# Two ordering ties on VectorE in a four-layer graph network: ranking steps behind the expert's additions, and a combine's later additions behind the first normalised nodes

## The chip, the cores and the metric

The kernel runs on one core of one Trainium2 chip. The metric is the device time of one execution in microseconds (us), as the median of several. One core has five engines that run their own instruction streams in order: TensorE (PE in the profile; its weight loads are listed as PEld), VectorE (DVE), ScalarE (ACT), GpSimd (POOL) and SyncE (SP), which here only issues transfers. They wait for one another by semaphores. ScalarE and GpSimd issue transfers as well. Matrix products land in PSUM, in a pool of eight tiles that is shared by the whole program.

## The reference, cut to what matters

The graph has 3125 nodes with 256 features and 50000 weighted edges, sorted by destination. Four pairs of layers follow one another, each pair a graph convolution and a feed-forward layer. With `A[dst, src]` the sum of the edge weights and `C[dst, src]` the number of edges between two nodes, the parts that the change touches are these:

```
x = A @ (x @ W) + b                            # convolution 0

w   = x @ wr + br                              # gated expert layer (0)
sel = the 1561 nodes with the largest w        # of equal ones the lower index
y   = gelu(x @ w1 + b1) @ w2 + b2
x   = x + (w * y where sel, 0 elsewhere)

h   = norm(x) @ W_pre ...                      # convolution 1: two products with C,
                                               # scaled by the degrees
x   = x + ...; top-2 of 8 experts; x = x + z0 + z1   # feed-forward layer 1

h   = norm(x)                                  # convolution 2: four products with A
...
```

Ahead of each convolution but the first, `x` is normalised by layer norm without gain: each node's mean is subtracted and the result is divided by its standard deviation. In layer 1 each node goes to two experts; `z0` and `z1` are the two weighted results, a row of 256 values per node each. Further layers (three and the rest of two) aren't touched.

## The kernel before, in words

**Data.** The nodes are 25 tiles of 128 (`NT`; the last holds 53 nodes). `x` stays in SBUF with nodes on the partitions. `CHUNKS` are groups of four node tiles: six of four and one of one. GpSimd builds dense 3200 x 3200 tables of `A` (`tw`) and `C` (`tcn`) in DRAM by indirect scatters (L595), a few hundred each; those of `tcn` run through the gated expert layer and beyond, to 904.8 us. A convolution streams the table from DRAM through SyncE's queue and multiplies it with `h` (L265 where the result has features on the partitions, L305 where it has nodes there). The program holds two arms for edges that are sorted or not; here the sorted one runs.

**The gated expert layer** (`l0_ffn`, from L967). Here *all* nodes go through the expert, and the selection is applied afterwards. For each group, `expert` (L933) does the following.

- Eight hidden blocks: two matmuls (L941) into one PSUM tile, four passes in the trace's count, then the Gelu (L945) on ScalarE.
- One product per node tile: eight matmuls (64 in the trace for four tiles, L952), then `take`, which is the addition `y = ps + b2` on VectorE (L1016). It hands the PSUM tile back.

Beside it runs the generator `ranks` (L994). For each of the 25 node tiles it counts how many nodes of all have a larger `w`: two or three comparisons over a row of 3200 with an accumulated sum (L1000), and one over 128 for ties (L1004). `expert` takes a step of it at two of the eight hidden blocks and at two of the four node tiles; what is left over after the last group is run there. The sum (L1009) and the gate `s` (L1010) follow, and then 25 updates of `x` (L1022), one for each node tile. VectorE has all of these in one queue. `self.pace` hands the last addition of a group to the generator of the scatters: the next portion of GpSimd's scatters is tied behind it.

**From there to the second convolution** (`l1_gnn`, L1056). `norm` (L173) works in fives of node tiles: statistics (L163 and L164), the root on ScalarE (L168, tied behind the last Gelu), the reciprocal (L171) and five normalisations (L184). For each group, TensorE then transposes (L225), VectorE and ScalarE copy (L230, L232), TensorE projects (L345), VectorE adds a bias (L1074), ScalarE scales (L1075), and `split` (L317 to L319) makes the high and low parts with which L265 multiplies the first table.

**The combine** (end of `Experts.tiles`, from L2012). The two results per node lie in DRAM (`L_ffn_z`). Nine parts of 1, 1, 2, 4, 4, 4, 4, 4 and 1 node tiles are fetched on ScalarE's queue (L2023) into a ring of three buffers, `zt`. Two additions per part (L2039) put them on `x`; then `part` of `norm_parts` (L189) computes statistics (L201, L202), the root on ScalarE (L203), the reciprocal (L204) and the normalisations (L206). The third convolution, `spmm_rows` (L287), multiplies them with the table `tw`, node tile by node tile (L305). Its table loads after the first are tied behind the transfers of the parts whose nodes they serve.

**What sets the order.** The source order isn't the order of the engines' queues. A scheduler in the framework places each instruction by its estimate of when it can start, under the dependencies that it knows. `order(a, b, sync=False)` adds one such dependency by hand: `a` is placed after `b`. Between two instructions of one engine it needs no semaphore and only fixes their order in the queue.

Of the kernel before, what the change touches and what calls it, by code (L numbers as in the profile page):

```python
# [60 lines left out]
class Net:  # L61
# [127 lines left out]
    def norm_parts(self, name):  # L189

        nc, got, loads = self.nc, [], {}

        def part(t0, nt, load):
            loads[t0 + nt] = load
            if not got:
                got.append(self.nm_tile(name))
            mv = self.small.tile([P, 4, 2], F32, tag="mv4", name=self.name("mv"))
            rs = self.small.tile([P, 4], F32, tag="rs4", name=self.name("rs"))
            for i in range(nt):
                st = self.small.tile([P, 6], F32, tag="bn", name=self.name("bn"), bufs=4)  # L200
                nc.vector.bn_stats(st, self.x[:, t0 + i, :])  # L201
                nc.vector.bn_aggr(mv[:, i, :], st)  # L202
            nc.scalar.activation(rs[:, :nt], mv[:, :nt, 1], AF.Sqrt, bias=self.eps)  # L203
            nc.vector.reciprocal(rs[:, :nt], rs[:, :nt])  # L204
            for i in range(nt):
                nc.vector.tensor_scalar(  # L206
                    got[0][:, t0 + i, :],
                    self.x[:, t0 + i, :],
                    mv[:, i, 0:1],
                    rs[:, i : i + 1],  # L210
                    op0=ALU.subtract,
                    op1=ALU.mult,
                )

        return lambda: (got[0], loads), part

# [750 lines left out]
    def l0_ffn(self, fm, w, w1, w2):  # L967

        nc, ins = self.nc, self.ins
        ht = 8  # L970
        take_k = max(1, int(0.5 * N))
        take_k = take_k - 1 if take_k > 1 else 1
        with self.reusing("l0f") as pool:
            b1 = self.columns(pool, ins["L0_ffn_b1"].rearrange("(r p) -> r p", p=P), ht)
            b2 = pool.tile([P, D], F32, name="b2")
            nc.sync.dma_start(b2, ins["L0_ffn_b2"].partition_broadcast(P))


            wp, low = pool.tile([P, NT], F32, name="score_p"), pool.tile([P, NT], F32, name="low")
            nc.vector.tensor_scalar(low, self.valid, -1.0, FMAX, op0=ALU.add, op1=ALU.mult)  # L980
            nc.vector.tensor_mul(wp, w, self.valid)
            nc.vector.tensor_add(wp, wp, low)
            row = pool.tile([P, NP], F32, name="score_row")
            self.broadcast_row(wp, row)

            after = pool.tile([P, P], F32, name="after")
            nc.vector.tensor_add(after, self.before, self.ident)
            nc.vector.tensor_scalar(after, after, 0.5, None, op0=ALU.is_lt)
            rk = pool.tile([P, NT, 4], F32, name="rk")
            nc.vector.memset(rk, 0.0)  # L990
            junk = pool.tile([P, NP], BF16, name="junk")
            rank, s = pool.tile([P, NT], F32, name="rank"), pool.tile([P, NT], F32, name="take")

            def ranks():  # L994
                for t in range(NT):
                    a, b = t * P, (t + 1) * P
                    me = wp[:, t : t + 1]
                    for i, (lo, hi, op) in enumerate(((0, a, ALU.is_ge), (b, NP, ALU.is_gt), (a, b, ALU.is_gt))):
                        if hi > lo:
                            nc.vector.tensor_scalar(  # L1000
                                junk[:, lo:hi], row[:, lo:hi], me, None, op0=op, op1=ALU.add,
                                accum_out=rk[:, t, i : i + 1],
                            )
                    nc.vector.scalar_tensor_tensor(  # L1004
                        junk[:, a:b], row[:, a:b], me, after, op0=ALU.is_equal, op1=ALU.mult,
                        accum_out=rk[:, t, 3:4],
                    )
                    yield
                nc.vector.tensor_reduce(rank, rk, AX.X, ALU.add)  # L1009
                nc.vector.scalar_tensor_tensor(s, rank, float(take_k), w, op0=ALU.is_lt, op1=ALU.mult)  # L1010

            y, steps, taken = self.nm_tile("y"), ranks(), []
            for t0, nt in CHUNKS:
                last = self.expert(
                    pool, fm[:, :, t0 * P : (t0 + nt) * P], nt * P, w1, b1, AF.Gelu_apprx_tanh, ht, w2,
                    lambda i, ps: taken.append(nc.vector.tensor_add(y[:, t0 + i, :], ps, b2)), steps,  # L1016
                )
                self.pace(taken[-1])
            for _ in steps:
                pass  # L1020
            for t in range(NT):
                nc.vector.scalar_tensor_tensor(  # L1022
                    self.x[:, t, :], y[:, t, :], s[:, t : t + 1], self.x[:, t, :], op0=ALU.mult, op1=ALU.add
                )
        return last
# [242 lines left out]
    def prefix(self, pool, t, n):  # L1268
# [7 lines left out]
        return t  # L1276

    def slot_owners(self, pool, slots, tiles):


# [10 lines left out]
        hot = self.nm_tile("hot").rearrange("p t d -> p (t d)").bitcast(BF16)  # L1291
        place = hot[:, : n * P].rearrange("p (n c) -> p n c", c=P)
        which = hot[:, n * P : n * (P + 2 * tiles)].rearrange("p (n s c) -> p n s c", s=2, c=tiles)
        ps = self.psum()[:, : 2 * tiles]
        step = 10 if n % 10 == 0 else 5
# [165 lines left out]
    def l3_ffn(self, late):  # L1461
# [54 lines left out]
        def rest():  # L1516
            with self.reusing("l3f") as pool:
# [36 lines left out]
                nc.vector.scalar_tensor_tensor(slot, slot, -none, kept, op0=ALU.add, op1=ALU.mult)  # L1554
                nc.vector.tensor_scalar(slot, slot, none, None, op0=ALU.add)
                number, place = self.slot_owners(pool, slot, NE * tiles)
                at, more = tile_("at", [P, NE * tiles]), tile_("more", [P, NE * tiles])
                of, to = tile_("of", [P, NE * tiles], I32), tile_("to", [P, NE * tiles], I32)
# [108 lines left out]
class Experts:  # L1667
# [253 lines left out]
    def tiles(self, pool, side, then):  # L1921
        net, nc, ins, tc = self.net, self.nc, self.ins, self.net.tc
# [45 lines left out]
        for i in range(STILES):  # L1968
# [40 lines left out]
            outs.append(st)  # L2009
            next(side, None)  # L2010

        bounds, back = [0, 1, 2] + list(range(4, NT, 4)) + [NT], []  # L2012
        if not summed:
            zt3 = net.nm_tile("zt")
            zts = [zt3[:, 8 * i : 8 * i + 8, :].rearrange("p (k t) d -> p k t d", k=2) for i in range(3)]
        for t0, t1 in zip(bounds, bounds[1:]):
            nt = t1 - t0
            x = net.x[:, t0:t1, :]
            full = nt if t1 < NT else nt - 1

            def fetch(dst, k):
                eng = nc.gpsimd if summed and t0 >= 2 else nc.scalar
                put = lambda d, s: back.append(eng.dma_start(d, s))  # L2023
                if full:
                    r = k * NP + t0 * P
                    put(dst[:, :full, :], z[r : r + full * P, :].rearrange("(t p) d -> p t d", p=P))
                if full < nt:
                    r = k * NP + (NT - 1) * P
                    put(dst[:TAIL, full, :], z[r : r + TAIL, :])

            if summed:
                fetch(x, 0)
            else:
                zt = zts[bounds.index(t0) % 3]
                for k in range(2):
                    fetch(zt[:, k], k)
                n = TAIL if full < nt else P
                for k in range(2):
                    nc.vector.tensor_add(x[:n], x[:n], zt[:n, k, :nt, :])  # L2039
            if then is not None:  # L2040
                then(t0, nt, back[-1])


@with_exitstack
# [61 lines left out]
```

## Time and profile before

Three runs took 3753.24, 3747.77 and 3751.30 us: median 3751.3. The profile is of another execution.

| Of the profiled execution | us | share or note |
|---|---|---|
| its time | 3749.16 | |
| its span, first to last instruction | 3747.4 | mean granted clock of TensorE 0.953 |
| TensorE busy (PE) | 3483.3 | 93% |
| its weight loads (PEld, beside the matmuls) | 2635.7 | 70% |
| VectorE busy | 1324.5 | 35% |
| GpSimd busy | 1055.8 | 28% |
| ScalarE busy | 788.5 | 21% |
| gated expert layer | 205.95 | 624.85 to 830.80 from the span's start; TensorE busy 184.17, clock 0.93 |
| from there to the first product with `tcn` | 32.99 | 830.80 to 863.79; TensorE busy 29.30 |
| combine ahead of the third convolution | 50.00 | 1490 to 1540; TensorE busy 33.52, clock 0.83 |

Busy time adds the time in which an engine had an instruction under way; the engines overlap, so that the sum says nothing, and what counts is how long each one idles and for whom. The list of waits names for each engine the line that waited, the engine and line that released it, the total, how often and the longest. The timeline shows runs of equal instructions with start and duration, and in brackets the idle time before them with the one who ended it. `x20` is a count. The granted clock is the share of full clock that TensorE was given.

### The profile page before, as it was taken

To read this page: it belongs to the slowest core of one execution; us is meant where nothing else is said; L and a number is where in the kernel's file an instruction comes from. 1 tells how busy PE (TensorE), PEld (TensorE's weight loads), DVE (VectorE), ACT (ScalarE), POOL (GpSimd) and SP (SyncE) were. 2 spreads that over 40 slices of the span, in tenths; PEclk is the share of its full clock that TensorE was granted. 3 is DMA by queue.
4 is the path that set the end of the run, shared out by engine and by line. 5 is a ranking of instruction groups with operands and counts; after the bars stand their busy time and mean duration, and the time that the engine had idled before them with its cause. 6 is when DMAs were issued, how large, how long until landed. Compare 5 with 4: busy or idle time off the path is not lost. (4 is left out here: it accounts for less than half of the span.)

```text
span 3747.4 us, 45864 instructions
## 1 busy us (share of the span) xinstructions
PE 3483.3 (93%) x16848; PEld 2635.7 (70%) x16848; DVE 1324.5 (35%) x4523; ACT 788.5 (21%) x1748; POOL 1055.8 (28%) x1020
## 2 busy tenths in 40 slices
PE   6779999799999698999999999999999989999698
PEld 5557786468877598788444888444799987877344
DVE  9975628933125533300000000124521127323334
ACT  3321002122112244000000000011344445222232
POOL 5777777776000254000000000000233330000232
PEclk7759999899999899999999999999999999999799
DMA  8789650016676598743542543543444567676440
GB/s 325 284 265 328 223 165 18 1 43 182 211 249 215 176 323 260 238 149 124 179 144 91 196 149 124 178 158 122 115 110 116 171 211 240 230 254 216 89 102 24
DMA packets 430038, 655.67 MB, mean 175 GB/s; under 512 B 62929, under 2 KB 206057, under 8 KB 429804
## 3 DMA queue, kind: packets, MB, share of 16 engines
q1 hardware_dynamic: 351150, 567.87, 45.5%
q0 software_dynamic: 48560, 50.07, 6.0%
q10 hardware_dynamic: 30094, 34.70, 2.8%
q8 instruction: 135, 2.21, 0.2%
q14 instruction: 99, 0.81, 0.1%
HBM read 622.05 MB, written 128.56 MB: 200 GB/s over the span
## 5 line engine op out<-in xcount | busy, mean ns | idle before, releaser
L265 PE MATMUL ps<-tt,h 128*128 128x512 f32 (+1 forms) x2800 | 1074.0, 466 | 16.3 <-ACT h L318 13.7
L265 PEld LDWEIGHTS ps<-tt,h 128*128 128x128 f32 x2800 | 514.5, 190 | 358.6 <-issue 288.9
L1980 PE MATMUL ps<-xe,w 128*128 128x128 f32 x2688 | 323.7, 277 | 8.2 <-DVE xe L1960 7.6
L1980 PEld LDWEIGHTS ps<-xe,w 128*128 128x128 f32 x2688 | 319.0, 193 | 17.0 <-DVE xe L1960 8.6
L1989 PE MATMUL ps<-w,hid 128*128 128x256 f32 x1344 | 312.6, 383 | 0.0
L595 POOL DMA_INDIRECT tcn<-cnt,idx_c x285 | 283.4, 994 | 86.9 <-issue 85.7
L895 PE MATMUL ps<-hw,tt 128*128 128x256 f32 x1250 | 289.3, 390 | 16.7 <-DMA tt<-tw 12.8
L595 POOL DMA_INDIRECT tw<-tot,idx_w x273 | 266.8, 977 | 83.2 <-issue 81.7
L305 PE MATMUL ps<-n,tt 128*128 128x256 f32 x1250 | 274.3, 383 | 16.5 <-DVE n L206 16.5
L1248 POOL DMA_DIRECT2D L_ffn_z<-x x5 | 3.8, 765 | 977.7 <-DVE bn L1187 901.7
L895 PEld LDWEIGHTS ps<-hw,tt 128*128 128x128 f32 x1250 | 240.0, 195 | 51.0 <-issue 13.3
L305 PEld LDWEIGHTS ps<-n,tt 128*128 128x128 f32 x1250 | 240.1, 192 | 50.6 <-DVE n L206 17.3
L305 PE MATMUL ps<-h,tt 128*128 128x256 f32 x1250 | 270.0, 379 | 0.0
L1989 PEld LDWEIGHTS ps<-w,hid 128*128 128x128 f32 x1344 | 248.9, 192 | 29.8
L265 PE MATMUL ps<-tt,h_lo 128*128 128x512 f32 (+1 forms) x700 | 260.9, 380 | 0.0
L265 PE MATMUL ps<-tt,lo 128*128 128x512 f32 (+1 forms) x700 | 260.6, 380 | 0.0
L305 PEld LDWEIGHTS ps<-h,tt 128*128 128x128 f32 x1250 | 237.5, 190 | 32.3
L1983 ACT ACTIVATE hid<-ps,par 128x128 f32<-128x128 f32 x672 | 225.5, 364 | 160.0 <-PE ps L1980 131.3
L1997 POOL DMA_INDIRECT L_ffn_z<-yb,to x112 | 149.0, 1330 | 322.5 <-ACT hid L1983 201.8
L345 PE MATMUL ps<-w,fmc 128*128 128x256 f32 x700 | 172.6, 400 | 17.4 <-ACT fmc L1084 13.8
L1141 DVE TENSOR_SCALAR h<-ps 128x256 f32<-128x256 f32 x24 | 10.2, 426 | 479.8 <-PE ps L305 479.8
L547 DVE SCALAR_TENSOR_TENSOR eq<-cells,dinv_row,ahead 128x256 bf16<-128x256 f32 (+3 forms) x391 | 179.3, 516 | 0.0
(408 smaller groups left out, 3951.0 us busy)
## 6 DMA issues: line engine op xcount, KB each, us to landing
tt<-tw SPq DMA_DIRECT2D x120, 1280.0 KB
tt<-tcn SPq DMA_DIRECT2D x119, 1280.0 KB
w<-in_L_ffn_W SPq DMA_DIRECT2D x112, 1024.0 KB
w<-in_L_ffn_W SPq DMA_DIRECT2D x112, 512.0 KB
tw<-zero_row SPq DMA_DIRECT2D x23, 1600.0 KB
tt<-tw SPq DMA_DIRECT2D x36, 768.0 KB
tcn<-zero_row SPq DMA_DIRECT2D x13, 1472.0 KB
w<-in_L_ffn_w SPq DMA_DIRECT2D x18, 1024.0 KB
```

The lines of the kernel that those rows point to most:

```text
L265: nc.tensor.matmul(pair[m], lhsT=part[:, k, m * P : (m + 1) * P], rhs=tt[:, j, :].bitcast(dt), start=k == 0 and i == 0, stop=k == NT - 1 a ...
L305: nc.tensor.matmul(ps[i], lhsT=tt[:, j, i * P : (i + 1) * P], rhs=h[:, k, :], start=k == 0, stop=k == NT - 1)
L345: self.nc.tensor.matmul(ps, lhsT=fm[:, k, i * P : (i + 1) * P], rhs=w[:, k, :], start=k == 0, stop=row is None and k == KD - 1)
L547: nc.vector.scalar_tensor_tensor(eqs[j], cells[k][:, at : at + m], self.col["w"][:, j : j + 1], ahead[:, GROUP * P - m :], op0=ALU.is_equa ...
L595: st = nc.gpsimd.indirect_dma_start(out=table[:, :], out_offset=bass.IndirectOffsetOnAxis(ap=idx[:, c : c + 1], axis=0), in_=src[:, c, :], ...
L895: nc.tensor.matmul(ps[:, i * D : (i + 1) * D], lhsT=tt[:, j - a, (i0 + i) * P : (i0 + i + 1) * P], rhs=hw[:, j, :], start=j == a, stop=j = ...
L1141: nc.vector.tensor_scalar(new[:, t, :], ps, 0.5, None, op0=ALU.mult)
L1248: put(dst[t0 * P : (t0 + full) * P, :].rearrange("(t p) d -> p t d", p=P), src[:, :full, :])
L1980: nc.tensor.matmul(ps, lhsT=w1[:, k, h * P : (h + 1) * P], rhs=xe[:, k, :], start=k == 0, stop=k == KD - 1)
L1983: nc.scalar.activation(hid[:, h, :], ps, func, bias=par[:, h : h + 1])
L1989: nc.tensor.matmul(ps, lhsT=hid[:, h, :], rhs=w2[:, h, :], start=h == 0, stop=h == ht - 1)
L1997: st = nc.gpsimd.indirect_dma_start(out=z[:, :], out_offset=bass.IndirectOffsetOnAxis(ap=self.to[ph][:, 0, j : j + 1], axis=0), in_=yb, in ...
```

## The change

It has two parts, both in the order of VectorE's instructions; no computation, buffer or transfer is added or removed.

In `ranks`, each comparison of a ranking step is placed behind the last addition L1016 that the source has emitted by then (`taken[-1]`, where there is one). The list `taken` is moved ahead of the generator.

In the combine, `part` returns its last normalisation, and the list `ready` collects these. From the third part on, each addition L2039 is placed behind one of them: those of the third part (node tiles 2 and 3) behind the normalisation of the first part (tile 0), those of all later parts behind that of the second (tile 1).

```diff
@@ norm_parts.part
             for i in range(nt):
-                nc.vector.tensor_scalar(
+                last = nc.vector.tensor_scalar(
                     got[0][:, t0 + i, :],
...
                 )
+            return last
@@ l0_ffn
+            taken = []
+
             def ranks():
                 for t in range(NT):
...
                         if hi > lo:
-                            nc.vector.tensor_scalar(
+                            one = nc.vector.tensor_scalar(
                                 junk[:, lo:hi], row[:, lo:hi], me, None, op0=op, op1=ALU.add,
                                 accum_out=rk[:, t, i : i + 1],
                             )
+                            if taken:
+                                self.order(one, taken[-1], "the experts' results are needed first", sync=False)
...
-            y, steps, taken = self.nm_tile("y"), ranks(), []
+            y, steps = self.nm_tile("y"), ranks()
@@ Experts.tiles
+        ready = []
         bounds, back = [0, 1, 2] + list(range(4, NT, 4)) + [NT], []
...
                 for k in range(2):
-                    nc.vector.tensor_add(x[:n], x[:n], zt[:n, k, :nt, :])
+                    add = nc.vector.tensor_add(x[:n], x[:n], zt[:n, k, :nt, :])
+                    if len(ready) > 1:
+                        net.order(add, ready[min(len(ready) - 2, 1)], "the first nodes are needed first", sync=False)
             if then is not None:
-                then(t0, nt, back[-1])
+                ready.append(then(t0, nt, back[-1]))
```

## The prediction

> **What bounds the kernel now.** I read the page first: TensorE is busy 93% of a span of 3747.4 us, so time is won only where it idles or runs at a lower clock. The list of waits then shows which idle time belongs to a line of the diff, and the timelines of these two places show the price. Times below are us from the span's start; *group* is one entry of CHUNKS (four node tiles), *part* is one of the nine pieces of the combine.
>
> The ranking. TensorE's timeline over the second and third group of the gated expert layer; columns are start, duration, line, operation, count, and in brackets the idle time before it and who ended it:
>
> ```profile
> 652.54 8.75 PE L941 MATMUL ps<-fm,w 128*128 128x512 f32 x20
> 661.72 1.98 PE L941 MATMUL ps<-fm,w 128*128 128x512 f32 x4 [0.43 <-DVE y L1016]
> 667.78 3.78 PE L941 MATMUL ps<-fm,w 128*128 128x512 f32 x4 [4.08 <-DVE y L1016]
> 673.86 3.78 PE L941 MATMUL ps<-fm,w 128*128 128x512 f32 x4 [2.29 <-DVE y L1016]
> 677.43 15.13 PE L952 MATMUL ps<-w,hid 128*128 128x256 f32 x64
> 692.39 7.03 PE L941 MATMUL ps<-fm,w 128*128 128x512 f32 x16
> 703.58 3.68 PE L941 MATMUL ps<-fm,w 128*128 128x512 f32 x4 [4.15 <-DVE y L1016]
> 710.85 3.47 PE L941 MATMUL ps<-fm,w 128*128 128x512 f32 x4 [3.59 <-DVE y L1016]
> 715.18 1.98 PE L941 MATMUL ps<-fm,w 128*128 128x512 f32 x4 [0.86 <-DVE y L1016]
> 723.53 3.78 PE L941 MATMUL ps<-fm,w 128*128 128x512 f32 x4 [6.36 <-DVE y L1016]
> ```
>
> Seven times TensorE waits for an addition of L1016, 21.8 us in all, because VectorE has that addition queued among ranking work (621 to 728) and the PSUM tile is not handed back. Four matmuls take 1.98 after a short wait and 3.5 to 3.8 after a long one: the clock drops as well. The table by stage has the sum (columns: stretch, its length, busy time of TensorE, its weight loads, VectorE, ScalarE, GpSimd, granted clock, DMA):
>
> ```profile
> 652.54:692.39 39.85, 33.04 (x97) 19.96 (x96) 39.85 (x85) 5.50 (x8) 30.40 (x32) 0.83 0.02 1
> 692.39:741.14 48.75, 33.78 (x98) 19.66 (x97) 46.49 (x108) 5.50 (x8) 37.17 (x39) 0.86 0.02 1
> 741.14:768.68 27.54, 27.54 (x97) 18.24 (x96) 6.11 (x16) 5.50 (x8) 21.02 (x22) 1.00 0.02 1
> ```
>
> The first two groups cost 39.85 and 48.75, an undisturbed one 27.54: 33.5 us of waits and slow clock. After 741 VectorE is nearly idle, and there the updates of x (L1022) and the statistics (L163) of early nodes run for nothing.
>
> The combine. TensorE, then VectorE, ahead of the third convolution:
>
> ```profile
> 1504.28 9.58 PE L305 MATMUL ps<-n,tt 128*128 128x256 f32 x32 [14.05 <-DVE n L206]
> 1516.30 3.95 PE L305 MATMUL ps<-n,tt 128*128 128x256 f32 x10 [2.44 <-DVE n L206]
> ```
> ```profile
> 1511.55 1.22 DVE L2039 TENSOR_TENSOR x<-x,zt 128x1024 f32<-128x1024 f32 x1 [2.11 <-DMA zt<-L_ffn_z]
> 1512.69 0.17 DVE L204 RECIPROCAL rs<-rs 128x4 f32<-128x4 f32 x1
> 1514.70 1.23 DVE L2039 TENSOR_TENSOR x<-x,zt 128x1024 f32<-128x1024 f32 x1 [1.83 <-DMA zt<-L_ffn_z]
> 1515.84 1.38 DVE L206 TENSOR_SCALAR n<-x,mv,rs 128x256 f32<-128x256 f32 x4
> ```
>
> TensorE starts at node tile 0's normalised value, does four tiles and waits for tile 4, which stands behind two additions whose transfers are late.
>
> **What the skill says.** The Trainium skill, "PSUM — Partial Sum Buffer", section "Engine vs sequencer instructions": VectorE is strict FIFO and matmuls start in program order; the waits above are that. "TensorE: Matmul & The Clock Gate", section "What's actually happening": half clock after about 3.4 us of idleness, full clock after as much work. The trace agrees roughly: 3.78 against 1.74 for four matmuls (13.9 us for 32 in undisturbed groups). "DMA: Bandwidth & Descriptors", section "Queues, rings and completion order": the queues of SP and ACT take turns on the same 16 engines. Here ACT's queue moves 0.69 MB in 1502 to 1504 alone, but 0.24 MB in 1508 to 1510 beside SP's 0.52.
>
> **Ranking, step by step.** In the built order the additions stand between the ranking steps, and SP and GpSimd keep their order.
>
> 1. *Removed.* A step costs VectorE about 4.2 (106 us of L1000 to L1004 over 25). An addition is now at most one step late, and its PSUM buffer is needed again only eight allocations later, at least 10 us on. All seven waits go: the layer's matmuls end at 830.8 - 33.5 = 797.3.
> 2. *What that exposes.* Step 23 follows the addition of tile 22 (group six: 786.9 + 0.2 + 0.35) and takes 4.0; the addition of tile 23 follows, and step 24 (3.9) ends at 795.6. L1009 and L1010 take 0.5. Only now can x change. VectorE does in line: 25 updates at 0.396 (8 from 728.17 to 731.34) = 9.9; the last addition 0.33; 25 statistics with aggregate at 0.39 = 9.8; four reciprocals 0.5; 20 normalisations at 0.34 (five in 1.70 at 829.92) = 6.8; and 0.6 to 0.7 for small waits between. It reaches the first copy L230 at about 824 and ends it at 824.7. Before, it ended at 838.5: 13.8 gained of 33.5.
> 3. *Given back.* TensorE now idles from 797 to about 812, and again about 7 us before that copy, so the next 20 L345 matmuls (4.58 at 838.58) start at half clock: +2.2. And the built order puts each group's copy L230 behind four additions L1074, where it stood ahead of them; TensorE, which needs 4.85 a group here, waits for it about 0.4, in some four groups, and 0.3 at the first: +1.9.
>
> So the second convolution's first matmul comes at 863.8 - 13.8 + 4.1 = 854.1: **-9.7**, bounds -7 (twice the give-back's uncertain half) and -13 (no give-back). From there to 1490 TensorE is the bound (25.0 of 25 us in most stretches). Its first matrix load, at 829.7, waits for TensorE's last matmuls of the layer and moves with them. GpSimd's scatters run back to back until 904.8; their ties to additions are met earlier, and by the code's own ranges the last loads that need them are due only near 970.
>
> **Combine.** Same additions, other order: tiles 2 and 3 are added after tile 0 is normalised, all later ones after tile 1. Reading the new VectorE order with these durations: tile 0 normalised at 1500.0 (was 1504.2), tile 1 at 1501.1; tiles 2 and 3 at about 1509.3 (were at 1507), as they now stand behind three large additions; tile 4 at 1513.5 (was 1516.2), as ScalarE's queue issues two of its transfers about 4 us earlier, ahead of a root. TensorE does two tiles slowly, waits about 3, does two more, and takes tile 4 at about 1514.0, not 1516.3: **-2.3**. The transfers were not seen in this order: bounds -4.5 (no wait for tiles 2 and 3) and +2 (SP's matrix loads, now released earlier, take the engines from them). Later tiles are close to due (tile 12 at 1529, needed 1528.4), so I take -2.3.
>
> Sum: -12.0. The profiled execution took 3749.2 for a span of 3747.4 and would take 3737.2. The median is 2.1 above it, so I forecast **3739.3**.
>
> **Rivals.**
>
> *The gain is lost on the way.* In the second convolution a matrix load issued at 904.78 is waited for at 914.29. If loads are held by the scatters' traffic until 905 whatever TensorE does, it waits there for what it gained: only -2 remains, 3749. For it: that one wait. Against it: the list shows 0.6 us of such waits in all.
>
> *The exposed tail is longer.* My tail uses start-to-start times of pipelined runs. If each instruction, now in another mix, takes its mean duration, it is 25 x (484 + 416 + 176) + 20 x 413 ns = 35.2 in place of 26.5. If the copies and L1074 stretch likewise (some 4) and the combine gives +2, it comes to -9.7 + 8.7 + 4 + 2 = +5: 3756. The new order decides against the kernel once the tail takes about 10 us more than I say. Against it: the same instructions already mix at 731 to 735 and 829 to 838 at my rate.
>
> *It does nothing.* The ties carry no semaphore. But the built order does show additions and steps alternating, so little is left for 3751.
>
> **How the numbers follow.** Forecast 0.74 (own range 3733 to 3744); lost on the way 0.14; longer tail 0.09; nothing 0.03. 0.2% (7.5 us) is about what a measurement of this kernel can tell from no change. Almost all of the first case is beyond it: faster 0.76, same 0.15, slower 0.09. The range runs from 3732 (no give-back, -13, and -4.5, with a little for the median) to 3748, which leaves the upper part of the second case and the third out.
>
> **What would show it.** No waits of L941 on L1016, and groups of 27.5; the last expert matmul near 797; L1022 in one run from about 796; TensorE idle some 15 us after 797 and the first tcn matmul near 854; the first L305 near 1500 with a wait for tile 2 near 1509. Wrong, if the first tcn matmul comes after 860, if L265 then waits for DMA by several us, or if L305 resumes after 1516 less what was gained before.

## The result, and the profile after

| | median us | range | runs |
|---|---|---|---|
| before | 3751.3 | 3747.77 to 3755.51 | 7 |
| changed | 3739.17 | 3734.59 to 3745.28 | 7 |

The ratio is 0.9967, with a 95% interval of 0.9957 to 0.9977: 9 to 16 us of 3751. The profiled execution took 3745.28 us for a span of 3743.5 and was the slowest of its seven, so the two spans differ by only 3.9. Stages have to be compared instead.

**The ranking.** TensorE's timeline over the same stretch as before (start, duration, line, operation, count). The added lines shift the numbers: L163 to L206 stand where they stood, L226 to L953 one further, L1015 to L1080 five further.

```profile
653.31 13.90 PE L942 MATMUL ps<-fm,w 128*128 128x512 f32 x32
667.04 13.98 PE L953 MATMUL ps<-w,hid 128*128 128x256 f32 x64
680.85 13.90 PE L942 MATMUL ps<-fm,w 128*128 128x512 f32 x32
694.59 13.98 PE L953 MATMUL ps<-w,hid 128*128 128x256 f32 x64
```

No wait and no slow block is left. The table by stage for the same two stretches (stretch, length, TensorE, weight loads, VectorE, ScalarE, GpSimd, clock, DMA):

```profile
652.54:692.39 39.85, 39.85 (x128) 24.03 (x127) 28.07 (x59) 9.62 (x14) 30.23 (x32) 1.00 0.02 1
692.39:741.14 48.75, 48.75 (x179) 33.67 (x178) 31.02 (x61) 8.25 (x12) 37.18 (x39) 1.00 0.02 1
```

TensorE is busy throughout, at full clock, where it was busy 33.04 and 33.78.

What came in its place stands behind the layer. VectorE, then TensorE:

```profile
796.99 0.24 DVE L1015 SCALAR_TENSOR_TENSOR take<-rank,score 128x25 f32<-128x25 f32 x1
797.27 4.44 DVE L1027 SCALAR_TENSOR_TENSOR x<-y,take,x 128x256 f32<-128x256 f32 x11
801.63 0.42 DVE L1021 TENSOR_TENSOR y<-ps,b 128x256 f32<-128x256 f32 x1
801.97 5.62 DVE L1027 SCALAR_TENSOR_TENSOR x<-y,take,x 128x256 f32<-128x256 f32 x14
807.51 0.74 DVE L163 BATCH_NORM_STATS2 bn<-x 128x6 f32<-128x256 f32 x2
```
```profile
794.61 3.62 PE L953 MATMUL ps<-w,hid 128*128 128x256 f32 x16
812.40 2.18 PE L226 MATMUL ps<-ident,n 128*128 128x128 f32 x8 [14.18 <-DVE n L184]
814.62 3.12 PE L346 MATMUL ps<-wf,fmc 128*128 128x256 f32 x8
817.57 1.04 PE L226 MATMUL ps<-ident,n 128*128 128x128 f32 x8
818.85 1.13 PE L346 MATMUL ps<-wf,fmc 128*128 128x256 f32 x4 [0.24 <-ACT fmc L233]
825.02 7.31 PE L346 MATMUL ps<-wf,fmc 128*128 128x256 f32 x20 [5.04 <-DVE fmc L231]
...
839.95 5.41 PE L346 MATMUL ps<-wf,fmc 128*128 128x256 f32 x16 [1.85 <-ACT fmc L233]
...
856.69 0.59 PE L266 MATMUL ps<-tt,h 128*128 128x512 f32 x1
```

The 25 updates start only when the last ranking step is done. TensorE idles 14.18 and 5.04 us, and two blocks then run slowly: 7.31 for 20 matmuls that took 4.58 before, 5.41 for 16 that take 3.72 in the other groups. The first product with `tcn` comes at 856.69 (863.79 before).

**The combine**, ahead of the third convolution:

```profile
1494.48 6.23 PE L306 MATMUL ps<-n,tt 128*128 128x256 f32 x16 [9.88 <-DVE n L206]
1502.98 12.31 PE L306 MATMUL ps<-n,tt 128*128 128x256 f32 x48 [2.27 <-DVE n L206]
1516.41 3.94 PE L306 MATMUL ps<-n,tt 128*128 128x256 f32 x17 [1.12 <-DVE n L206]
```

TensorE starts after 9.88 idle us (14.05 before), does two node tiles, waits 2.27 for tile 2, then runs to tile 7 and waits 1.12 for tile 8.

### The profile page after: what moved, and what is told of

Same layout as the page of the kernel before. It is cut to its first block, busy times and chain, and to the rows that moved or that the text cites. A ratio compares the mean times of both kernels' runs of the same rounds, so it can differ in the third digit from the quotient of the medians.

```text
span 3743.5 us, 45864 instructions
## 1 busy us (share of the span) xinstructions
PE 3478.8 (93%) x16848; PEld 2633.1 (70%) x16848; DVE 1334.1 (36%) x4523; ACT 791.4 (21%) x1748; POOL 1063.0 (28%) x1020
## 5 line engine op out<-in xcount | busy, mean ns | idle before, releaser
L266 PE MATMUL ps<-tt,h 128*128 128x512 f32 (+1 forms) x2800 | 1073.9, 466 | 16.3 <-ACT h L319 15.2
L266 PEld LDWEIGHTS ps<-tt,h 128*128 128x128 f32 x2800 | 514.8, 190 | 359.2 <-issue 289.1
L306 PE MATMUL ps<-n,tt 128*128 128x256 f32 x1250 | 274.8, 383 | 13.3 <-DVE n L206 13.3
L306 PEld LDWEIGHTS ps<-n,tt 128*128 128x128 f32 x1250 | 240.3, 192 | 47.8 <-DVE n L206 14.5
L306 PE MATMUL ps<-h,tt 128*128 128x256 f32 x1250 | 270.0, 379 | 0.0
L266 PE MATMUL ps<-tt,lo 128*128 128x512 f32 (+1 forms) x700 | 261.1, 380 | 0.0
L266 PE MATMUL ps<-tt,h_lo 128*128 128x512 f32 (+1 forms) x700 | 260.4, 379 | 0.0
L306 PEld LDWEIGHTS ps<-h,tt 128*128 128x128 f32 x1250 | 237.5, 190 | 32.3
L346 PE MATMUL ps<-w,fmc 128*128 128x256 f32 x700 | 172.9, 400 | 16.2 <-ACT fmc L1089 12.7
```

The lines of the kernel that those rows point to most:

```text
L266: nc.tensor.matmul(pair[m], lhsT=part[:, k, m * P : (m + 1) * P], rhs=tt[:, j, :].bitcast(dt), start=k == 0 and i == 0, stop=k == NT - 1 a ...
L306: nc.tensor.matmul(ps[i], lhsT=tt[:, j, i * P : (i + 1) * P], rhs=h[:, k, :], start=k == 0, stop=k == NT - 1)
L346: self.nc.tensor.matmul(ps, lhsT=fm[:, k, i * P : (i + 1) * P], rhs=w[:, k, :], start=k == 0, stop=row is None and k == KD - 1)
```

## The experiments

The runs fell on several chips. On one, the kernel before takes 3753; on three others it takes 4194 to 4198, and there the engines lose time through the first third of the span in waits that the profile puts down to no instruction or transfer ("issue", "remote"). In the first 1000 us of one such trace of the kernel before, TensorE loses 99.0 us to "issue" at L895 alone, in the first convolution, and VectorE 183.7 to "remote" at L905. From the first product with `tcn` to TensorE's last instruction, that trace takes 2874 us, the one on a faster chip 2868. The two kinds are told apart below by the time of the kernel before.

To set stages against each other whatever came ahead of them, two distances were read from every trace. *A* runs from the first expert matmul (L942) to the first product with `tcn` (L266); *B* from the last expert matmul ahead of the combine to the first VectorE result of the third convolution's first group.

| before takes 3751 to 3753 | A | B |
|---|---|---|
| before | 238.94 | 63.29 |
| changed | 230.97 | 60.61 |
| ranking tie alone | 228.04 | 61.34 |
| changed, combine part by part | 230.85 | 62.29 |
| changed, ranking spread | 206.82 | 59.85 |

| before takes 4194 to 4198 | A | B |
|---|---|---|
| before, two traces | 284.92, 285.59 | 63.34, 62.99 |
| combine tie alone, three | 289.98, 286.45, 293.01 | 59.99, 60.16, 60.80 |
| ranking tie alone | 295.78 | 62.21 |
| changed, two | 296.40, 291.80 | 60.38, 60.49 |
| changed, ranking spread | 311.96 | 59.97 |

### Each part alone

The ranking tie alone: the changed kernel without

```diff
-                    if len(ready) > 1:
-                        net.order(add, ready[min(len(ready) - 2, 1)], "the first nodes are needed first", sync=False)
```

> The ranking tie alone. My theory: it carries -9.7 of the forecast (the changed kernel's trace has the first tcn matmul at 856.7 where it was 863.8, and later about -7.5 to -9.7 between 900 and 1350): about 3741.5 us, ratio 0.9974; no wait of L942 on the addition; the combine as before, with a first wait of L306 of about 14 us and a second one of 2.4 us ahead of node tile 4. Rival (the ranking's gain is lost on the way and the combine carries the change): 3749 to 3751.

On a chip where the kernel before takes 4196 it took 4199.18, ratio 1.0005 (0.9993 to 1.0017). Neither theory had that. On another chip:

> The ranking tie alone, on another chip than the first time, where everything took 4190 us. My theory: about 3742 where before takes 3751, ratio 0.9975; in the trace the combine as before. Rival (the combine carries the change): 3749 to 3751.

Where before took 3753.01 it took 3740.99, ratio 0.9966 (0.9955 to 0.9977). The first theory holds: the ranking carries the change. Alone it measured -12.0 where -9.7 was expected, as much as the whole change, so these times don't show what the combine adds. Its combine waits as that of before, ahead of tile 0 and then 2.60 us (2.44 before) ahead of tile 4:

```profile
1492.51 9.07 PE L306 MATMUL ps<-n,tt 128*128 128x256 f32 x32 [13.97 <-DVE n L206]
```

The combine tie alone: the changed kernel without

```diff
-                            if taken:
-                                self.order(one, taken[-1], "the experts' results are needed first", sync=False)
```

> The combine tie alone. My theory: -2.3 (the changed kernel's trace shows -2.7 from before the combine to after it): about 3749 us, ratio 0.9994, hardly to be told from no change; the first L306 some 4 us after where it now idles less (wait 9.9 in place of 14.0), then a wait of about 2.3 for node tile 2. Rival (the combine carries most): 3742 or less. The seven waits of L942 on the addition are back, 21.8 us.

> The combine tie alone, where before takes some 3752 us. My theory: from the last expert matmul ahead of the combine to the first result of the third convolution's first group 60.2 us in place of 62.5 (means of four traces with the tie and four without), idle time ahead of the first L306 of 9 to 10 in place of 14; the time is 2.3 less, ratio 0.9994. From the first expert matmul L942 to the first product with tcn, 238.9 us as before. Rival (more than this comes from the combine): ratio below 0.9985.

> The combine tie alone, a third time, for a chip on which before takes 3752 us. Its ranking is that of the kernel before, so the trace also repeats the kernel before up to the combine. On such a chip: 238 to 240 us from the first L942 to the first product with tcn, 21 to 22 us of waits of L942 on the addition; 60.2 us in the combine in place of 62.5; ratio 0.9994. On a chip where before takes 4190: 286 to 290 us, 60.2 us, ratio 0.9994 within its interval.

All three ran on chips of the slower kind: ratios 0.9998 (0.9986 to 1.001), 1.0003 (0.9991 to 1.0015) and 1.0006 (0.9993 to 1.0019). 2.3 us can't be seen in such times, but B shows it: over all traces, 59.85 to 60.80 with the tie (eight, mean 60.28), 61.34 to 63.34 without either order of the combine (five, mean 62.63), no overlap, **-2.35**.

This mean mixes two things. One is what the tie acts on, the waits of L306: in B they sum to 15.8 to 17.2 us without the tie and 11.9 to 15.6 with it, -3.0 in the mean. The other is TensorE's busy time, 44.8 to 47.3 without and 44.9 to 48.3 with it, depending on how many products run slowly. Like pairs differ accordingly: -2.8 with the ranking in the order of before (63.17 to 60.32, slower chips), -1.8 with the ranking tie in both (62.21 to 60.44, slower chips), -0.7 on the faster kind (61.34 to 60.61, one trace each). So the sign and the shorter waits are shown, and the size only roughly. The time of the combine tie alone on a chip of the faster kind was not measured.

### The changed kernel and the kernel before again

> The changed kernel once more, for a second trace of it. 3739, ratio 0.9967. Its first trace lost 4 us again between 1380 and 1460 (expert weights waited for, 3.5 us) and 4 us between 3440 and 3520 (no added wait). If that is what the change triggers, both stand in this trace too, at the same places with the same size; if it is chance of an execution, they differ, and the shift against before stays near -10 to the end.

> The changed kernel once more. 3739 to 3741 us, ratio 0.9967. From the first L942 to the first product with tcn 228 to 231 us (231.0 in its first trace, 228.0 with the ranking tie alone, though VectorE's order there is the same; the slow blocks of L346 differ: if that is chance of the clock, this trace lies anywhere between).

> The kernel before once more, for a second trace of it. 3748 to 3755 us. Against the first trace of it: shifts of up to some 4 us at places with transfers waited for or at a drop of the clock if these are chance; under 1 us everywhere if they are not.

> The kernel before once more, for a second trace where it takes some 3752 us: 238 to 240 us from the first expert matmul to the first product with tcn, and 62 to 63.5 in the combine.

All four ran on slower chips, so neither kernel has a second trace on a faster one. The changed kernel took 4194.88 and 4195.83, ratios 0.9999 (0.9990 to 1.0008) and 0.9999 (0.9986 to 1.0011): **on these chips the change wins nothing that can be measured.** The traces show why for the ranking. The list of TensorE's waits within the expert layer (line, who ended it, total, how often, longest; waits over 1 us in total), before and changed:

```profile
PE ps L952 <- ACT hid L945: 21.0, 3, 9.3
PE ps L941 <- issue: 10.7, 10, 1.9
PE ps L952 <- issue: 7.6, 6, 1.7
PE ps L941 <- DVE y L1016: 6.4, 1, 6.4
```
```profile
PE ps L953 <- issue: 22.1, 23, 1.7
PE ps L953 <- ACT hid L946: 18.7, 4, 7.8
```

The wait that the tie removes is only 6.4 here (5.2 to 6.6 in the five traces without the tie), beside much longer ones for other things, and the waits without a visible cause grow from 18.3 to 22.1 (16.3 to 18.9 in the five, 20.3 to 22.1 in the three with it). The layer takes as long with the tie (233.4 to 235.6) as without (234.2 to 237.1), and the tail behind it is exposed all the same: A is 291.8 to 296.4 in those three (mean 294.7) and 284.9 to 293.0 in the five (288.0). There the ranking tie costs some 7 us of A; the combine gains 1.8 to 2.8, and the times can't tell the sum from nothing. Why engines stall so on these chips, and whether it is the chips themselves or their state at the time, wasn't settled; the packets of the busiest transfer queue take 78 ns in the mean on both kinds.

### Where the rest of the 33.5 us went

If the tail of VectorE takes what the waits gave, an earlier end of the ranking must give it back. Three ranking steps to every two places at which the expert takes one:

```diff
                         accum_out=rk[:, t, 3:4],
                     )
-                    yield
+                    if t % 3 != 1:
+                        yield
```

> The changed kernel with three ranking steps to every two places at which the expert takes one: 25.2 of ranking and 1.7 us of additions in a group of 27.5, so the ranking ends in the fifth group, near 745 from the start of the span in place of 797, and updates and statistics follow each addition. My theory (what is left of the 33.5 us went to the exposed tail of VectorE: updates, statistics, normalisations after the last ranking step, and to what it costs TensorE when it idles): first tcn matmul near 831 in place of 856.7, no idle time of 14 us ahead of the first transposes, about -25 against the changed kernel: 3714 us, 3709 to 3725. Rival (loads of tcn are held by the scatters until about 911, and TensorE waits for them for what it gained): 3730 to 3739, with several us of waits of L266 on DMA. Rival (VectorE gets over-full and the additions come late again): waits of L942 on the addition, 3725 to 3745.

3717.16, where before took 3753.01: ratio **0.9895** (0.9878 to 0.9912). The last step ended at 745.4, and behind the layer TensorE goes on at once:

```profile
794.65 3.62 PE L953 MATMUL ps<-w,hid 128*128 128x256 f32 x16
798.11 1.33 PE L226 MATMUL ps<-ident,n 128*128 128x128 f32 x8
...
805.83 6.16 PE L346 MATMUL ps<-wf,fmc 128*128 128x256 f32 x20 [1.92 <-DVE fmc L231]
```

A is 206.82, 24.2 below the changed kernel and 32.1 below before: the exposed tail, with its two idle times and slow blocks, was what the ranking tie left of the 33.5. Both rivals fall. L942 doesn't wait for the addition, and L266 waits 0.4 us for transfers, although it starts 24 us earlier while the scatters still end at 911. This version beats the kernel before on that chip. The changed kernel wasn't timed beside it; by their ratios to before (0.9895 and 0.9967, intervals that don't overlap) it beats that one too.

> The ranking spread three steps to two places, beside the changed kernel on the same chip: 3717 us, ratio to before 0.990, some 22 us under the changed kernel. From the first L942 to the first product with tcn 206 to 208 us.

This ran on a slower chip, where it *lost*: 4210.7, ratio 1.0031 (1.0018 to 1.0044). In its trace the expert layer itself takes 253.9 us, with 41.9 us of waits for the Gelus, and ScalarE loses 44.2 us there to "issue" and 31.7 to "remote" (12.7 and 15.5 in a trace of the changed kernel on the same chip). Why the spread ranking meets more of that than the changed kernel stays open. So it is shown to be the better kernel only where the program takes 3750.

### The combine, part by part

```diff
-                    if len(ready) > 1:
-                        net.order(add, ready[min(len(ready) - 2, 1)], "the first nodes are needed first", sync=False)
+                    if ready:
+                        net.order(add, ready[-1], "the first nodes are needed first", sync=False)
```

> The changed kernel with every addition of the combine behind the last normalisation of the part before it, so that node tiles 2 and 3 no longer stand behind the larger additions. Theory A (the order costs the wait of 2.3 us for tile 2, and what bounds later parts is also the order): no wait for tile 2, tile 8 earlier too, -2 to -3 against the changed kernel in the trace. Theory B (tiles from 8 on are bound by their transfers): no wait for tile 2, but the wait for tile 8 grows by as much, and TensorE takes it up again at the same time: within 0.7 us of the changed kernel, about 3739 us. If the strict order makes VectorE slower than TensorE's 7.4 us a part: waits for each part, +2 to +8.

3740.69, ratio to before 0.9966 (0.9951 to 0.9981), and B 62.29, 1.7 above the changed kernel. TensorE:

```profile
1486.29 9.65 PE L306 MATMUL ps<-n,tt 128*128 128x256 f32 x32 [9.04 <-DVE n L206]
1497.54 1.99 PE L306 MATMUL ps<-n,tt 128*128 128x256 f32 x8 [1.60 <-DVE n L206]
1502.84 0.76 PE L306 MATMUL ps<-n,tt 128*128 128x256 f32 x1 [3.31 <-DMA tt<-tw]
```

The wait for tile 2 is gone, as both theories had it, but a matrix load is then waited for, 3.31 us. Theory A falls. B is right that the gain is given back to transfers, and wrong on the place: not tile 8's own, but a table load. In the code such loads are tied behind the fetches of the parts; that this tie made the load late wasn't tried. Of the 1.7 above the changed kernel, 0.7 are waits (13.95 in place of 13.27 in all), and the rest is busy time at a lower clock. There is one trace of it.

## Why the prediction was right

The forecast of 3739.3 met 3739.2, and the sum of -12.0 met -12.1. The mechanism was right: the waits went, the tail of VectorE was exposed in their place, and the difference was left. That the two numbers agree within 0.2 is luck. In the changed kernel's own trace A and B together fell by 10.7, and only 3.9 was left at the end of it; the ranking tie alone measured -12.0, where the sum has -9.7 for it; and each of these intervals is some 8 us wide. The steps:

1. *Removed.* All seven waits went and the slow blocks with them. The layer's matmuls end at 798.23, with the layer begun 0.87 later than in the trace of before: 797.4, where 797.3 was forecast.
2. *What that exposes.* The last step ends at 796.66 (forecast 795.6), the 25 updates follow in a row, TensorE idles until 812.4 (forecast about 812), and the first copy ends at 824.97 (forecast 824.7). All of these include the 0.87; without it the copy is 14.4 earlier than before (forecast 13.8).
3. *Given back* was mis-sized: 4.1 forecast, 6.45 measured. From the end of the first copy to the first product with `tcn` it took 25.27 before and 31.72 after. The terms: 2.73 for the 20 slow matmuls (forecast 2.2); 1.69 for a second slow block of 16, which the forecast didn't have; 2.03 for the waits for copies (forecast 1.9). The last term was met by luck: the forecast had VectorE's copy late by 0.4 in four groups, and measured are two waits, 1.85 and 0.66, that ScalarE's copy ended; it stands behind four scalings L1080 in ScalarE's queue. TensorE idled 5.04 ahead of the 20 matmuls (forecast about 7), but its idle time alone doesn't set the clock of such a block: behind 1.90 us it took 4.58 in the kernel before, behind 1.92 us 6.16 with the ranking spread. The trace of the ranking tie alone, with the same order on VectorE in this stretch, has only 3.65, and that of the part-by-part combine 6.45: how many blocks run slowly varies from one execution to the next. A fell by 8.0, 10.9 and 8.1 in the three traces against the one trace of before, within the bounds of -7 and -13 and by 9.0 in the mean.
4. *"From there TensorE is the bound"* holds only roughly. In the changed kernel's trace the gain was 7.5 us at 920 to 1030 and 9.4 from 1060 on: what the kernel before did from 1020 to 1070, in 50.0 us, took 48.1 (48.2 to 50.3 in the other traces, with either order); between 1380 and 1480 some 4 were lost, where the second layer's experts wait 3.5 us for their weights (0.2 before). The other traces have 0 to 3.1 us of these waits with the ranking tie and 0 to 1.4 without it, so whether the change brings some of them isn't settled. After the combine the gain stood at 8.3; 3.2 more were lost at 3445 to 3452, where matmuls of 0.28 us took 0.41 behind a wait of 1.43 us that the kernel before has as well. Eleven of the fourteen traces have such a loss at this place, two of the three of the kernel before among them, so it isn't the change's. Whether these losses made this execution the slowest of its seven isn't shown, as the other six have no trace.
5. *Scatters "back to back until 904.8"* was wrong: the last one starts at 910.6, not at 904.8. The gap between the two traces grows by 4.6 of these 5.8 us in one long scatter beside the row of updates (last section). It cost nothing, as L266 waited for no load of `tcn` up to 1060.
6. *The combine:* -2.3 forecast, -2.35 measured over thirteen traces, and -0.7 to -2.8 by like pairs, so that the close agreement is chance here too. In the changed kernel's trace the idle time ahead of tile 0 fell by 4.2 (forecast 4.2), and the wait for tile 2 is 2.27 (forecast about 3). The wait for tile 8 was not in the sum.

The rivals. *The gain is lost on the way* didn't happen at the place it named: TensorE waited 0.6 us at most for matrix loads up to 1060, even where it came 24 us earlier. On the slower chips the gain is absent, but there the traces show something else: other waits fill the layer, and the tail is exposed. *The exposed tail is longer* fell: VectorE kept its pace, 0.40 an update. *It does nothing* fell, on the chip of the forecast. The prediction said nothing of other chips, and should be read as one for a chip on which the program takes 3751.

## What to carry to other kernels

When work is moved from ahead of a bound engine to behind something else, follow the moved work to its own consumer: here the ranking's end gates 25 updates and all that follows, so that unblocking TensorE during the layer was worth 33.5 us but delivered 8 to 11 up to the next product, and setting the *rate* of the side work, so that it neither blocks nor ends late, delivered 32 on the faster chip. Compare stages by distances within a trace, and their waits apart from their busy time: some 2 us can be seen there that times which vary by 8 don't show. A schedule that wins on one chip can lose on another; measure on more than one.

## What the runs showed of the hardware

GpSimd's scatters slow down while VectorE runs updates of `x` in a row. GpSimd in the changed kernel (start, duration, line):

```profile
797.01 0.97 POOL L596 DMA_INDIRECT tcn<-cnt,idx_c  x1 [0.30 <-issue]
798.29 1.10 POOL L596 DMA_INDIRECT tcn<-cnt,idx_c  x1 [0.30 <-issue]
799.69 1.28 POOL L596 DMA_INDIRECT tcn<-cnt,idx_c  x1 [0.30 <-issue]
801.28 1.28 POOL L596 DMA_INDIRECT tcn<-cnt,idx_c  x1 [0.30 <-issue]
802.86 5.57 POOL L596 DMA_INDIRECT tcn<-cnt,idx_c  x1 [0.30 <-issue]
808.74 0.97 POOL L596 DMA_INDIRECT tcn<-cnt,idx_c  x1 [0.30 <-issue]
```

The 25 updates run from 797.27 to 807.59. Two scatters take 1.28 in place of 0.97 meanwhile, and the last one takes 5.57 and ends 0.84 after the row does. With the ranking spread, 16 updates run in a row from 746.07 to 752.49, and a scatter of 3.26 us ends at 753.34, 0.85 after it. In the traces of the ranking tie alone and of the part-by-part combine, the last scatters beside the row take 4.04 and 5.57 and end 0.83 and 0.85 after it. The row of 8 updates in the kernel before (728.17 to 731.42) has none longer than 1.28. What the two engines share there wasn't tried.
